# A graph attention layer on one core: address reads behind the copies, norms a round later, eight column tiles more

## The chip, the cores and the metric

The kernel runs on one core of a Trainium2 chip. The metric is the device time of one execution in microseconds (us), as the median of several runs; lower is better. A profiled execution gives the trace, whose span runs from the first to the last instruction of the core.

The engines are named as in the profile: PE (TensorE, matmuls), PEld (its weight loads), DVE (VectorE), ACT (ScalarE), POOL (GpSimd, which here issues the gathers) and SP (SyncE, which issues the plain transfers). ACTq, DVEq and SPq are the sequencers of these engines: they read instructions in order, carry out register reads themselves, and hand the rest to the engine.

## The reference: what is computed

One layer of attention over a graph of 6250 nodes with 206250 edges, sorted by their destination, 128 features in 8 heads of 16:

```python
Q, K, V = x @ WQ, x @ WK, x @ WV            # 6250 x 128 each
Eh = edge_attr @ WE                         # 206250 x 128
score = sum over d of K[src] * Q[dst] * Eh / 4      # per edge and head
score = exp(clip(score, -5, 5))
wV = segment_sum(V[src] * score, dst)       # per node
Z  = segment_sum(score, dst)
out = layernorm(x + wV / (Z + 1e-6))
```

## The kernel before

**Tiles and rounds.** Edges are cut into 1612 tiles of 128 (one edge a partition), tiles into 406 batches of four (the last ones smaller). After a start in which the tables K and V of all nodes are made and written to memory (`kv`), one loop over `b` (line 626) has one round per batch. From batch 12 on (`XB`) the order of instructions on each engine is that in which the program writes them (line 628, `manual_schedule`), so a round's place in a queue can be read off the loop's body.

**What a round does.** Gathers: `gather` (line 421) fetches for each tile the rows of K and V of its 128 source nodes, one indirect DMA a tile, issued by POOL (line 430), 256 floats a row, into one of twelve `kvrows` buffers. The first gather of a batch waits for a matmul of an earlier batch (line 434, `lag`, from 12 batches at first down to 3 at the end), so that gathers keep to the pace of TensorE. TensorE: `stage_a` multiplies the edge features by WE (`eps`, line 498) and picks the rows of Q with a one-hot matrix (`qps`, line 501). DVE: `stage_b` of the batch before multiplies K by Q (`kq`, line 508) and by the edge features (`kqe`, 511), sums over each head (`sc`, 514) and clips (517); one-hot matrices are built (470 and 483) for two batches at a time. ACT: `weigh` takes the exponential twice (524 to `msg`, 525 to `exp_p`). DVE: `messages` multiplies V by `exp_p` (558), a round after `weigh`. TensorE: `stage_c` adds the messages by destination with a one-hot matmul (578).

**Column tiles.** For a share of the tiles POOL issues no gather (line 425). Their 128 source columns of x, which lies transposed in SBUF (`xT_sb`, 128 features by 6250 nodes), are copied one by one into a tile `xcol`, and a matmul with WK and WV makes the rows (`project_columns`, line 412), which ACT puts in the place of the gathered ones (line 419). `column_tiles` (line 75) says which: one batch in 13/6 on average from batch 24 on, `COLP = (13, 6)`, 176 in all. Each such batch has three gathers instead of four.

The copies are in `columns` (line 372). ACT takes columns 0 to 79 in ten runs of eight (`COLA = (8, 10)`), one copy a column (line 403), DVE columns 80 to 127 in six runs of eight, two columns an instruction (`COLV = (8, 6)`, line 400), so four instructions a run. Where a column lies is only known at run time: each run is preceded by a read of eight addresses from SBUF to registers of that engine's sequencer (line 392). `addresses` holds what is read and not yet used. A call tops it up to two runs and then copies one, so the read in front of a run is that of the run behind it. `columns` is called for ACT twice a round (lines 651 and 685: the first up to half a round's share, ahead of `weigh`; the second behind it) and for DVE three times (663, 669, 675), a run each at most.

**Norms.** When the sums of two blocks of 128 nodes are complete, `finish` (line 542) issues matmuls that put them together (`finps`), and in the same round, behind `weigh`, ACT copies the result out (`fin`, line 551) and appends the steps of `layernorm` to `pending`. At the next round `pending` goes to `norms` (line 653), and `fill` (line 616) issues one step at a time, four times a round on DVE, after the steps that make Q's table (`qwork`). The first step (`rz`, line 791) reads `fin`. When all steps are issued the output store goes on SP two rounds later.

Of the kernel before, what the change touches and what calls it, by code (L numbers as in the profile page):

```python
# [18 lines left out]
N, E, D, H, DH = 6250, 206250, 128, 8, 16  # L19
# [30 lines left out]
QLOOK = 3  # L50
QREG = 16
COL0 = 24
COLP = (13, 6)
COLA = (8, 10)
COLV = (8, 6)
COLL = 8
# [3 lines left out]
XT_AT = RING + P  # L60
# [14 lines left out]
def column_tiles():  # L75

    last = LAST // B - 1
    n = (last - 2 - COL0 + COLL) * COLP[1] // COLP[0]
    return [B * min(COL0 + k * COLP[0] // COLP[1], last - (n - 1 - k)) + B - 1 for k in range(n)]

# [22 lines left out]
def edge_attention(ctx: ExitStack, tc: tile.TileContext, x, xT, srcT, srcC, dstT, dstB, dst0, bnd, lo, eaT,  # L103
                   wq, wkv, we, out, kv, qtab, qs, relD):
    nc = tc.nc
# [27 lines left out]
    nbat = len(batches)  # L133
    col_batches = [t // B for t in column_tiles()]
    col_half = (len(col_batches) + 1) // 2
    col_at = cp.tile([col_half, 2, P], I32, name="col_at")
# [4 lines left out]
    with ExitStack() as fast:  # L141
# [79 lines left out]
        def late_loads():  # L221
            if NT > C0:
                nc.sync.dma_start(src_sb[1], srcT[:, C0:])
                nc.sync.dma_start(dst_sb[:, C0:], dstT[:, C0:])
# [72 lines left out]
        xbs, stores, norms, pending, ready, finished, loaded_x = {}, [], [], [], [], [], set()  # L297
# [39 lines left out]
        def load_rel(c):  # L337
            if c in rels or c * RC >= NT:
                return
            n = min(RC, NT - c * RC) * P  # L340
            rels[c] = wp.tile([QROWS, RC * P], BF16, name="relb", bufs=2)
            nc.sync.dma_start(rels[c][:, :n], relD.rearrange("j e -> (j e)")[None, c * RC * P:c * RC * P + n]
                              .to_broadcast([QROWS, n]))
# [3 lines left out]
        def load_chunk(c):  # L347
            if c in chunks or c * CH >= NT:
                return
            n = min(CH, NT - c * CH) * P  # L350
            tl = ep.tile([P, CH * P], F32, name="ea", tag="ea")
            nc.sync.dma_start(tl[:, :n], eaT[:, c * CH * P:c * CH * P + n])
            chunks[c] = tl
# [16 lines left out]
        addresses, fetched = {}, {}  # L370

        def columns(eng, b, share=1.0, most=99):

            size, runs = COLA if eng is nc.scalar else COLV
            first = 0 if eng is nc.scalar else COLA[0] * COLA[1]
            engine = mybir.EngineType.Activation if eng is nc.scalar else mybir.EngineType.DVE
            copy = eng.copy if eng is nc.scalar else eng.tensor_copy
            due = int((b - COL0 + COLL - 1 + share) * runs * COLP[1] / COLP[0] + 1e-6)
            total = len(col_batches) * runs
            while copied.get(engine, 0) < min(due, total) and most:  # L380
                most -= 1
                k, j = divmod(copied.get(engine, 0), runs)
                copied[engine] = copied.get(engine, 0) + 1
                if k not in col_tiles:
                    col_tiles[k] = wp.tile([P, P], F32, name="xcol", bufs=XCOLS)
                to, j = col_tiles[k].bitcast(U8), first + j * size
                known = addresses.setdefault(engine, [])
                while len(known) < 2 and fetched.get(engine, 0) < total:
                    kf, jf = divmod(fetched.get(engine, 0), runs)
                    fetched[engine] = fetched.get(engine, 0) + 1  # L390
                    jf = first + jf * size
                    known.append(nc.values_load_multi_w_load_instructions(  # L392
                        col_at[kf % col_half:kf % col_half + 1, kf // col_half, jf:jf + size], engines=(engine,),
                        min_val=XT_AT, max_val=XT_AT + 8 * (N - 1) + 4,
                        skip_runtime_bounds_check_because="edges name nodes")[1])
                at = known.pop(0)
                if eng is nc.vector:
                    for c in range(0, size, 2):
                        both = [xT_bytes[:, ds(a - XT_AT, 8)] for a in at[c:c + 2]]
                        eng.tensor_tensor(to[:, 4 * (j + c):4 * (j + c) + 8], *both, op=ALU.bitwise_or)  # L400
                    continue
                for c in range(size):
                    copy(to[:, 4 * (j + c):4 * (j + c) + 4], xT_bytes[:, ds(at[c] - XT_AT, 4)])  # L403

        def project_columns(b):

            if b not in col_batches:
                return
            g = gathered[b]
            k = col_batches.index(b)  # L410
            pk = psT.tile([P, 2 * D], F32, name="colkv", tag="oT")
            nc.tensor.matmul(pk, col_tiles.pop(k), wkv_sb, start=True, stop=True)  # L412
            projected.append((g, pk))

        def place_columns():

            while projected:
                g, pk = projected.pop()
                nc.scalar.copy(g[:, B - 1, :], pk)  # L419
# [202 lines left out]
            elif norms and (not late or late.pop()) and next(norms[0], None) is None:  # L622
                norms.pop(0)

        held, late = [], []
        for b in range(nbat + 3):
            if b >= XB and not manual:
                manual.append(fast.enter_context(tc.manual_schedule()))
            held += [(b + SLAG, store) for store in stores]
            stores.clear()  # L630
            if held and (held[0][0] <= b or b >= nbat):
                held.pop(0)[1]()
            if b < nbat:
                load_chunk(batches[b][0] // CH + EB - 3)
                load_rel(batches[b][0] // RC + 1)
                load_q(batches[b][0] // WT + QLOOK)
                g = gathered.pop(b)
                if b == min(XB, nbat - 1):
                    late_loads()
                if b == min(XB + 8, nbat - 1):  # L640
                    relative(C0, NT)
                if b >= 30:
                    next(second_half, None)
                if b == 0:
                    for i in range(AHEAD):
                        stage_0(i)
                        stage_0t(i)
                stage_a(b, g)
                if b + GLEAD < nbat and b + GLEAD not in gathered:
                    gathered[b + GLEAD] = gather(b + GLEAD)  # L650
                columns(nc.scalar, b, 0.5)
            late[:] = [False] * 9 + [True] if b >= nbat - 2 else []
            norms.extend(pending)
            pending.clear()
            for j in ready:
                finish(j)
            ready.clear()
            steps = stage_b(b - 1) if 0 <= b - 1 < nbat else iter(())
            next(steps, None)
            if b + AHEAD < nbat and together(b + AHEAD):  # L660
                stage_0(b + AHEAD)
            if b < nbat:
                columns(nc.vector, b, 1.0, 1)
            fill()
            next(steps, None)
            if b + AHEAD < nbat and together(b + AHEAD):
                stage_0t(b + AHEAD)
            if b < nbat:
                columns(nc.vector, b, 1.0, 1)
            fill()  # L670
            next(steps, None)
            if 0 <= b - 2 < nbat:
                messages(b - 2)
            if b < nbat:
                columns(nc.vector, b, 1.0, 1)
            fill()
            next(steps, None)
            fill()
            place_columns()
            if 0 <= b - 1 < nbat:  # L680
                weigh(b - 1)
            while blocks_out:
                blocks_out.pop(0)()
            if b < nbat:
                columns(nc.scalar, b)
            if 0 <= b - 2 < nbat:
                stage_c(b - 2)
            if b < nbat:
                project_columns(b + GLEAD)
                build_q(q_built(min(NJ - 1, batches[b][0] // WT + QLOOK + 2)), True)  # L690
                if not qwork and len(built) < q_built(
                        min(NJ - 1, batches[min(nbat - 1, b + 3)][0] // WT + QLOOK + 2)):
                    qwork.append(q_rows(len(built)))
                    next(qwork[0])
                    fresh[:] = [0, 0, 0]
            if b == min(60, nbat):
                count_inside()
            if b == min(80, nbat + 1):
                inside = nc.values_load(cnt_i[0:1, 0:1], min_val=0, max_val=2 * EPAD,
                                        skip_runtime_bounds_check_because="two counts of EPAD edges")  # L700
# [158 lines left out]
```

## Time and profile before

| | us |
|---|---|
| median of three runs | 1847.12 (1847.1 to 1848.22) |
| the profiled execution, its own time | 1840.47 |
| its span | 1838.7 |
| mean granted clock of TensorE | 0.931 of full |

The profile page gives for each engine its busy time, its share of the span and its instructions; then the chain of work that ended last, followed back from the end, as shares by engine. Groups of instructions have the form: line, engine, operation, output <- input, shape, count | busy time, mean ns of one | idle time of the engine just ahead of them, and what ended most of it ("issue": nothing that the profile shows). Copies and other short instructions overlap on their engine, so busy time divided by count is less than the mean of one. The lists of waits give total us, how often, and the longest. The timelines give start and length in us, and in brackets the idle time ahead of an instruction with its releaser; equal instructions that follow each other are merged (x40). Busy time by window has one row a stretch, with the engines' busy time and instruction counts.

### The profile page before, as it was taken

The numbers are of one execution on the slowest core, as the hardware profiler recorded it, in microseconds if no ns is written. First come the engines' busy times: TensorE is split into PE (matmuls) and PEld (weight loads), VectorE is DVE, ScalarE is ACT, GpSimd is POOL, SyncE is SP. The second block draws the span as 40 slices with busy tenths as digits, with TensorE's granted clock in tenths as the row PEclk, the third lists the DMA queues.
The fourth block names the chain that finished last, engine by engine and source line by source line (L and its number), as shares of the span: only waits on it lengthen the run. The fifth ranks groups of instructions, "written<-read, shape, count | busy, mean of one in ns | idle before, by whom it ended". The sixth has DMA issues, their size and how long they took to land.

```text
span 1838.7 us, 48927 instructions
## 1 busy us (share of the span) xinstructions
PE 1299.2 (71%) x9130; PEld 1118.7 (61%) x9130; DVE 1720.6 (94%) x7478; ACT 1608.3 (87%) x15268; POOL 1375.8 (75%) x1443
## 2 busy tenths in 40 slices
PE   6886667676676777776777667766767667766776
PEld 4776656565665666665666556655656656655665
DVE  5579999999999999999999999999999999999998
ACT  2339889899999999999999999999999999999994
POOL 6777777777777777777777777777777777777774
PEclk8999899889989899999899999999999999899989
DMA  8776667676776577677667766866876676667762
GB/s 281 231 228 199 192 183 225 194 205 196 211 221 202 177 224 216 182 208 221 202 199 213 226 192 183 241 198 180 241 213 191 192 229 194 203 185 232 217 191 77
DMA packets 170631, 376.74 MB, mean 205 GB/s; under 512 B 58423, under 2 KB 84369, under 8 KB 170315
## 3 DMA queue, kind: packets, MB, share of 16 engines
q0 software_dynamic: 68144, 185.10, 35.0%
q1 hardware_dynamic: 101031, 187.38, 33.9%
q14 instruction: 242, 1.98, 0.3%
q8 instruction: 74, 1.21, 0.3%
q10 hardware_dynamic: 1140, 1.06, 0.2%
HBM read 358.60 MB, written 14.81 MB: 203 GB/s over the span
## 4 chain that ended last, share of the span: by engine, by line
DVE 42%; DMA 17%; ACT 13%; PE 11%; issue 6%; DVEq 5%; POOL 4%; ACTq 2%; SPq 0%; POOLq 0%
DMA kvrows<-kv,src 14%; ACT xcol L403 11%; DVE xcol L400 8%; DVE kqe L511 6%; DVE kq L508 6%; DVE sc L514 6%; POOL kvrows L430 4%; DVEq L392 4%; DVE onehot L470 4%; PE eps L498 4%; DVE msg L558 4%; PE agg L578 3%; DVE onehotT L483 2%; ACTq L392 2%; DMA dB_sb<-dstB 1%
## 5 line engine op out<-in xcount | busy, mean ns | idle before, releaser
L430 POOL DMA_INDIRECT kvrows<-kv,src x1388 | 1328.6, 957 | 423.0 <-issue 313.0
L403 ACT COPY xcol<-xT_sb 128x4 uint8 x14080 | 1422.3, 191 | 60.5 <-issue 54.2
L498 PE MATMUL eps<-we_sb,ea 128*128 128x128 f32 x3224 | 488.9, 298 | 384.8 <-issue 182.7
L498 PEld LDWEIGHTS eps<-we_sb,ea 128*128 128x128 f32 x3224 | 425.0, 205 | 482.6 <-issue 353.7
L578 PE MATMUL agg<-msg,onehot 128*128 128x136 f32 x3224 | 526.0, 310 | 109.4 <-DVE msg L558 101.1
L578 PEld LDWEIGHTS agg<-msg,onehot 128*128 128x128 f32 x3224 | 447.0, 208 | 165.6 <-DVE msg L558 152.2
L400 DVE TENSOR_TENSOR xcol<-xT_sb 128x8 uint8 x4224 | 416.1, 156 | 8.7 <-issue 4.6
L508 DVE TENSOR_TENSOR kq<-kvrows,qps 128x512 f32<-128x512 f32 x406 | 274.0, 675 | 35.2 <-PE qps L501 17.1
L558 DVE TENSOR_TENSOR msg<-kvrows,exp_p 128x512 f32<-128x512 f32 x406 | 271.1, 668 | 7.5 <-ACT exp_p L525 7.5
L511 DVE TENSOR_TENSOR kqe<-kq,eps 128x512 f32<-128x512 f32 x406 | 272.3, 671 | 3.1 <-PE eps L498 2.6
L514 DVE TENSOR_REDUCE sc<-kqe 128x32 f32<-128x512 f32 x406 | 270.2, 665 | 0.5
L501 PE MATMUL qps<-qw,onehotT 126*128 126x128 bf16 x1612 | 166.6, 227 | 0.0
L524 ACT ACTIVATE msg<-sc 128x32 f32<-128x32 f32 x406 | 92.6, 228 | 72.0 <-DVE sc L517 64.5
L470 DVE TENSOR_TENSOR onehot<-iota_p,dst_sb 128x512 f32<-128x512 f32 (+2 forms) x206 | 137.5, 668 | 2.0 <-PE agg L578 2.0
L501 PEld LDWEIGHTS <-onehotT 126*128 126x128 bf16 x1612 | 132.9, 102 | 8.2
L412 PE MATMUL colkv<-wkv_sb,xcol 128*128 128x256 f32 x352 | 114.2, 409 | 0.8 <-ACT xcol L403 0.8
L483 DVE TENSOR_SCALAR onehotT<-relb,node 126x1024 bf16<-126x1024 bf16 (+2 forms) x206 | 100.0, 486 | 3.3 <-DMA relb<-relD 2.0
L517 DVE TENSOR_SCALAR sc<-sc 128x32 f32<-128x32 f32 x406 | 82.1, 202 | 0.3
L525 ACT ACTIVATE exp_p<-sc 128x32 f32<-128x32 f32 x406 | 73.7, 182 | 0.0
L419 ACT COPY kvrows<-colkv 128x256 f32<-128x256 f32 x176 | 63.8, 362 | 0.3 <-PE colkv L412 0.3
L430 POOL DMA_INDIRECT kvrows<-x,src x48 | 46.3, 964 | 22.5 <-issue 11.6
L412 PEld LDWEIGHTS colkv<-wkv_sb,xcol 128*128 128x128 f32 x352 | 59.7, 209 | 1.0 <-ACT xcol L403 1.0
(76 smaller groups left out, 537.3 us busy)
## 6 DMA issues: line engine op xcount, KB each, us to landing
ea<-eaT SPq DMA_DIRECT2D x201, 512.0 KB
relb<-relD SPq DMA_DIRECT2D x100, 504.0 KB
kvrows<-kv,src POOLq DMA_INDIRECT x1388
qw<-qs SPq DMA_DIRECT2D x202, 31.5 KB
kv<-kvst SPq DMA_DIRECT2D x12, 512.0 KB
qs<-qst SPq DMA_DIRECT2D x48, 96.0 KB
xst<-xT SPq DMA_DIRECT2D x12, 256.0 KB
xb<-x SPq DMA_DIRECT2D x24, 128.0 KB
```

The lines of the kernel that those rows point to most:

```text
L400: eng.tensor_tensor(to[:, 4 * (j + c):4 * (j + c) + 8], *both, op=ALU.bitwise_or)
L403: copy(to[:, 4 * (j + c):4 * (j + c) + 4], xT_bytes[:, ds(at[c] - XT_AT, 4)])
L412: nc.tensor.matmul(pk, col_tiles.pop(k), wkv_sb, start=True, stop=True)
L430: ins = nc.gpsimd.indirect_dma_start(out=g[:k, i, :f], out_offset=None, in_=rows, in_offset=bass.IndirectOffsetOnAxis(ap=src_col(t)[:k], a ...
L470: nc.vector.tensor_tensor(tl[:, HW:].rearrange("p (t n) -> p t n", n=P)[:, :n, :HW], iota_p[:, None, :].to_broadcast([P, n, HW]), rel[:, t ...
L498: nc.tensor.matmul(pe[:, i, :], ea[:, i * P:i * P + P], we_sb, start=True, stop=True)
L501: expanded[b] = nc.tensor.matmul(pq[:, i, :], ohT[:, i * P:i * P + P], loaded[t0 // WT], start=True, stop=True)
L508: nc.vector.tensor_tensor(t0[:, :n], g[:, :n, :D], pq[:, :n], op=ALU.mult)
L511: nc.vector.tensor_tensor(t1[:, :n], t0[:, :n], pe[:, :n], op=ALU.mult)
L514: nc.vector.tensor_reduce(sc[:, :n], t1[:, :n].rearrange("p b (h d) -> p b h d", h=H), axis=AX.X, op=ALU.add)
L558: nc.vector.tensor_tensor(m[:, :n, :D].rearrange("p b (h d) -> p b h d", h=H), g[:, :n, D:].rearrange("p b (h d) -> p b h d", h=H), exp_p[ ...
L578: nc.tensor.matmul(aggs[k][:, 0], oh[0][:, oh[1] + i * P:oh[1] + i * P + P], m[:, i, :], start=not final and t % (QUAD * G) == 0, stop=tail)
```

## The change

There are three edits, in `columns`, in the loop, and in one constant.

1. The share of column tiles goes from 6 batches in 13 to 15 in 31. By `column_tiles` this gives 184 tiles, where the old constant gives 176; the change's own short description says 183.
2. ACT's address reads: a call tops up to one run (which only reads something in the very first run), copies, and then reads the addresses of the next run. DVE keeps two.
3. A norm whose `fin` was copied in round b goes to `norms` at round b + 2 instead of b + 1, by way of a list `waiting`; in the last rounds (from `nbat - 3` on) it goes at once.

```diff
-COLP = (13, 6)
+COLP = (31, 15)
...
-                while len(known) < 2 and fetched.get(engine, 0) < total:
...
+                def fetch(ahead):
+                    while len(known) < ahead and fetched.get(engine, 0) < total:
...
+                fetch(2 if eng is nc.vector else 1)
                 at = known.pop(0)
                 if eng is nc.vector:
...
                 for c in range(size):
                     copy(to[:, 4 * (j + c):4 * (j + c) + 4], xT_bytes[:, ds(at[c] - XT_AT, 4)])
+                fetch(1)
...
-        held, late = [], []
+        held, late, waiting = [], [], []
...
-            norms.extend(pending)
+            norms.extend(waiting)
+            waiting[:] = pending
             pending.clear()
+            if b >= nbat - 3:
+                norms.extend(waiting)
+                waiting.clear()
```

More of the change, by code (lines that the diff above doesn't have):

```diff
@@ L387, in columns @@
                 known = addresses.setdefault(engine, [])
-                while len(known) < 2 and fetched.get(engine, 0) < total:
[L389 to L395, printed above, removed]
+                def fetch(ahead):
+                    while len(known) < ahead and fetched.get(engine, 0) < total:
+                        kf, jf = divmod(fetched.get(engine, 0), runs)
+                        fetched[engine] = fetched.get(engine, 0) + 1
+                        jf = first + jf * size
+                        known.append(nc.values_load_multi_w_load_instructions(
+                            col_at[kf % col_half:kf % col_half + 1, kf // col_half, jf:jf + size],
+                            engines=(engine,), min_val=XT_AT, max_val=XT_AT + 8 * (N - 1) + 4,
+                            skip_runtime_bounds_check_because="edges name nodes")[1])
+                fetch(2 if eng is nc.vector else 1)
                 at = known.pop(0)
```

## Prediction

> **What bounds the kernel now.** I began with the page, first with its busy times and the chain that ended last.
>
> ```profile
> PE 1299.2 (71%) x9130; PEld 1118.7 (61%) x9130; DVE 1720.6 (94%) x7478; ACT 1608.3 (87%) x15268; POOL 1375.8 (75%) x1443
> DVE 42%; DMA 17%; ACT 13%; PE 11%; issue 6%; DVEq 5%; POOL 4%; ACTq 2%; SPq 0%; POOLq 0%
> ```
>
> DVE looks like the bound, and POOL, at 75%, looks free. It isn't. The waits of POOL between 138 and 1790 us (the stage in which column tiles are made) show why: 30 different releasers, all with the same longest wait. The two largest:
>
> ```profile
> POOL kvrows L430 <- issue: 294.7, 967, 0.3
> POOL kvrows L430 <- DVE xcol L400: 18.9, 62, 0.3
> ```
>
> No gather ever waited over 0.3 us, whoever is named as its releaser. So the 0.3 us is a fixed cost between two gathers, and the names are coincidence. The timeline of POOL says the same in the middle and at the very end:
>
> ```profile
> 956.44 0.95 POOL L430 DMA_INDIRECT kvrows<-kv,src  x1 [0.30 <-issue]
> 957.70 0.95 POOL L430 DMA_INDIRECT kvrows<-kv,src  x1 [0.30 <-issue]
> ...
> 1808.53 0.95 POOL L430 DMA_INDIRECT kvrows<-kv,src  x1 [0.30 <-PE agg L578]
> 1811.03 0.95 POOL L430 DMA_INDIRECT kvrows<-kv,src  x1 [0.30 <-issue]
> 1821.04 0.91 POOL L430 DMA_INDIRECT kvrows<-kv,src  x1 [0.30 <-PE agg L578]
> ```
>
> A gather takes a slot of 1.26 us (957.70 - 956.44), and the slots follow each other without a hole to 1822 us, 17 us before the end. POOL is a queue that is full from beginning to end.
>
> DVE is the second bound. Batch 208 has its first multiply (kq) at 984.41, batch 400 at 1814.09; their last gathers are the rows at 957.70 and 1811.03 above.
>
> ```profile
> 984.41 0.67 DVE L508 TENSOR_TENSOR kq<-kvrows,qps 128x512 f32<-128x512 f32 x1
> 1814.09 0.69 DVE L508 TENSOR_TENSOR kq<-kvrows,qps 128x512 f32<-128x512 f32 x1
> ```
>
> POOL's lead is 26.7 us at batch 208 and 3.1 us at batch 400. DVE is the faster of the two by little, lives off a head start of the gathers, and has used it up just as the work ends. The busy times by stage fit (the first row is the whole column stage):
>
> ```profile
> core 0: us, PE busy (x) PEld busy (x) DVE busy (x) ACT busy (x) POOL busy (x), PEclk, DMA share, GB/s
> 138.00:1790.00 1652.00, 1162.42 (x8305) 1008.27 (x8303) 1595.02 (x7116) 1539.79 (x14932) 1253.13 (x1309) 0.93 0.70 205
> 900.00:1100.00 200.00, 141.22 (x1025) 121.59 (x1023) 195.97 (x882) 190.50 (x1858) 151.84 (x159) 0.95 0.72 212
> 1700.00:1790.00 90.00, 65.00 (x442) 56.61 (x440) 84.18 (x382) 84.72 (x826) 68.06 (x73) 0.89 0.71 204
> ```
>
> DVE is busy 98% in the middle and 94% at the end, where it waits for gathers. ACT has 112 us without work in 1652. What DVE and ACT wait for in the same stage:
>
> ```profile
> DVE kq L508 <- PE qps L501: 16.8, 28, 1.0
> DVE rz L791 <- ACT fin L551: 15.7, 16, 2.5
> DVE kq L508 <- DMA kvrows<-kv,src: 6.5, 6, 1.8
> ...
> ACT xcol L403 <- issue: 52.1, 184, 0.9
> ACT msg L524 <- DVE sc L517: 37.9, 58, 4.5
> ACT fin L551 <- PE finps L537: 10.9, 9, 2.4
> ```
>
> Only 6.5 us of DVE's time is waiting for gathered rows. With a POOL that never held it, DVE would end about 6.5 us sooner; with a DVE that cost nothing, POOL would still end where it does. So there are two sums, one for each, and the later decides.
>
> **The change part by part.** The instruction order of the changed kernel has 184 column projections, where the old one has 176 (352 matmul passes, two each). So 8 tiles more are filled by copies, and 8 gathers are gone.
>
> **POOL.** 8 slots of 1.26 us: 10.1 us. Nothing stands between the slots, so POOL ends 10.1 us sooner if nobody holds it back. Its first gathers are the same.
>
> **DVE, more columns.** A column tile has 6 runs of 4 instructions on DVE (48 columns, 2 an instruction, 4 instructions behind one address read), so 48 runs more.
>
> ```profile
> L400 DVE TENSOR_TENSOR xcol<-xT_sb 128x8 uint8 x4224 | 416.1, 156 | 8.7 <-issue 4.6
> ...
> 1003.64 0.68 DVE L558 TENSOR_TENSOR msg<-kvrows,exp_p 128x512 f32<-128x512 f32 x1
> 1004.24 0.39 DVE L400 TENSOR_TENSOR xcol<-xT_sb 128x8 uint8 x4
> 1004.54 0.17 DVE L517 TENSOR_SCALAR sc<-sc 128x32 f32<-128x32 f32 x1
> ```
>
> Start to start a run costs 0.30 us here (1004.24 to 1004.54); by the busy time it is 416.1/1056 = 0.39 us, of which some overlaps its neighbours. I take 0.33, nearer the row without overlap: 48 x 0.33 = 15.8 us (14.4 to 18.9). All of it lies on DVE's path, which has no holes. It is more than POOL gains: by this edit alone DVE would be late by 15.8 - 6.5 = 9.3 us.
>
> **DVE, the norms a round later.** The first instruction of a block's norm (rz, line 791) stands in DVE's queue one round behind the matmuls that finish the block, and reads a copy that ACT makes behind the exponentials of that round:
>
> ```profile
> 1385.64 0.19 ACT L525 ACTIVATE exp_p<-sc 128x32 f32<-128x32 f32 x1
> ...
> 1385.94 0.39 ACT L551 COPY fin<-finps 128x272 f32<-128x272 f32 x1
> 1386.36 0.17 DVE L791 TENSOR_SCALAR rz<-fin 128x16 f32<-128x16 f32 x1 [0.31 <-ACT fin L551]
> ...
> 1388.10 0.67 DVE L558 TENSOR_TENSOR msg<-kvrows,exp_p 128x512 f32<-128x512 f32 x1
> ```
>
> Sixteen of the 24 waited, 15.7 us in all, the longest 2.5 us. A round is 4.3 us (984.41 to 1814.09 is 829.7 us for 192 rounds), so one round more covers the longest wait, and the 15.7 us go: -15.7. The output stores behind the norms move a round later on SP's queue too, behind loads of a later round; no instruction before the end waits for a store, and the last rounds hand norms over at once as before. No cost. The bounds: -15.7, if ACT's lateness then meets no other instruction, and 0, if it does (third rival).
>
> **ACT, more columns.** 80 copies a tile:
>
> ```profile
> L403 ACT COPY xcol<-xT_sb 128x4 uint8 x14080 | 1422.3, 191 | 60.5 <-issue 54.2
> L419 ACT COPY kvrows<-colkv 128x256 f32<-128x256 f32 x176 | 63.8, 362 | 0.3 <-PE colkv L412 0.3
> ```
>
> 8 x 80 x 1422.3/14080 = 64.6 us and 8 x 0.36 = 2.9 us: 67.5 us into 112 us of idle time. 44 us are left, 39 after the span has shrunk by 5. But 52.1 us of the 112 are gaps ahead of the copies ("issue"), which are no free time unless the reads that cause them are hidden.
>
> **ACT, the address reads.** One such gap, with the reads of ACT's sequencer in the same window:
>
> ```profile
> 1051.20 0.23 ACT L524 ACTIVATE msg<-sc 128x32 f32<-128x32 f32 x1 [0.55 <-DVE sc L517]
> 1051.33 0.18 ACT L525 ACTIVATE exp_p<-sc 128x32 f32<-128x32 f32 x1
> 1051.83 4.05 ACT L403 COPY xcol<-xT_sb 128x4 uint8 x40 [0.31 <-issue]
> ...
> L392 ACTq TENSOR_LOAD <-col_at x1: 547/547/547, 1051.2 to 1051.2; - x1
> L392 ACTq TENSOR_LOAD <-col_at x1: 547/547/547, 1052.0 to 1052.0; - x1
> ```
>
> ACT had caught up, the sequencer had nothing queued, and the read of 0.55 us stood in front of copies whose addresses had been there for long. The second read, at 1052.0, shows no gap: 40 copies in 4.05 us is 0.10 each with four more reads between them. There eight copies (0.8 us) were queued ahead of the read. Behind the change the first eight copies follow the exponentials at once, and the first read has those eight to hide behind, as the second has now. The copies of a run then need a read that has only just ended, where today one whole run lies between; since the sequencer is held for the whole 0.55 us either way, I count no more for it. So the 52.1 us fall to near 0 (0 to 52.1 kept for the range). ACT keeps 39 us of slack, 2%.
>
> The Trainium skill (Advanced Engine Details and Errata, Sequencer and Instruction Queues, Sequencer Loop) says that further engine instructions can be read and queued while a control instruction executes. By that rule the read wouldn't hold the copies, the gap would have another cause and would stay where it is, and the sum would be that of the fourth case below; the row at 1051.83 speaks against it, since the copies start just when the read that began at 1051.2 has ended.
>
> **What tight ACT costs DVE.** DVE's msg multiply needs ACT's exponentials of the round before. The whole span has 7.5 us of that wait:
>
> ```profile
> DVE msg L558 <- ACT exp_p L525: 7.5, 10, 1.3
> ```
>
> With ACT at 98% it will come up now and then: I take 1, between 0 and 7.5.
>
> **The sum.** DVE: +15.8 - 15.7 - 6.5 (gathers are 10.1 us sooner, none of the six waits is over 1.8) + 1.0 = -5.4 us. POOL: -10.1 us. DVE is the later: span 1838.7 - 5.4 = 1833.3. The profiled execution took 1840.47 us, 1.8 over its span; the median of the three runs is 1847.12, 8.4 over it. I put the difference on the median: **1841.7 us**, 0.3% faster.
>
> **The rivals.** A difference under 0.2%, 3.7 us, can hardly be told from none.
>
> Second case: POOL stays the bound. It needs DVE to save over 4.7 us more, for instance from the 16.8 us of kq on qps (28 rounds in which DVE is too short for TensorE; a run more in the round covers 0.3 of a wait). For it speaks that DVE waits for rows at the end; against it, that the added runs fall into those rounds only by chance. Time: 1847.1 - 10.1 = 1837.0.
>
> Third case: the wait only moves. rz waits because ACT is late, and an ACT with 67.5 us more work stays late; what rz doesn't wait, msg waits half a round on. For it: ACT's slack shrinks to 2%. Against it: in the rows above exp_p was done 0.5 us before fin (1385.83 to 1386.33), and msg on DVE starts 1.7 us behind rz. All of it back: 15.8 - 6.5 = +9.3, 1856.4; half back: 1848.6. I write 1849.
>
> Fourth case, the slower side: the reads still show, and ACT becomes the bound. Place: each of the 1840 reads. It decides from 39/1840 = 0.02 us a read on; above that every further 0.01 us costs 18 us. With today's 52.1 us kept, ACT needs 1540 + 67.5 + 52.1 + 10.9 (its wait for finps) = 1670 us in a stage of 1652: +18, 1865 us. For it: ACT is near full and the slack is thin. Against it: the gapless 40 copies.
>
> **How the numbers follow.** The forecast 0.50, of which 0.42 faster by over 0.2% and 0.08 within it; POOL the bound 0.17, faster; the wait moves 0.20, 0.13 within and 0.07 slower; ACT the bound 0.13, slower. Faster 0.59, same 0.21, slower 0.20. The range reaches from just under POOL's floor, 1836.5, to 1852, which holds half of the wait come back and the dear end of the runs (18.9 and 7.5 in the sum give +4.2, 1851.3). It leaves out the fourth case and the upper third of the third: just under 0.2.
>
> **What would show it.** Right: rz no longer waits for fin; "issue" ahead of ACT's copies is under 10 us; gathers still come every 1.26 us, 1380 from kv; DVE's wait for kvrows is near 0 and POOL's lead at batch 400 is over 3.1 us. Wrong: msg waits for exp_p by more than 7.5 us in all (third); ACT 99% busy, or gaps inside long rows of copies (fourth); POOL waits above 0.3 us, which would mean that buffers or the pace set by TensorE hold it and its 10.1 us are not to be had; a mean gather above 0.957 us.

## The result, and the profile after

The changed kernel takes 1842.14 us (median of 11 runs, 1839.2 to 1846.08), the kernel before 1847.12 us (11 runs). The ratio is 0.9972, 95% interval 0.9964 to 0.9979: 5.0 us faster. The profiled execution took 1842.14 us, just its median, with a span of 1840.4; that of before, with 1838.7, had been 6.6 us under its own median. So the two profiles can't be subtracted span from span, and what follows compares what each shows inside.

The page of the changed kernel: the chain that ended last by engine, and the groups of gathers and of ACT's copies.

```profile
DVE 51%; DMA 16%; PE 9%; issue 7%; DVEq 5%; POOL 5%; SPq 0%; ACT 0%; POOLq 0%
...
L435 POOL DMA_INDIRECT kvrows<-kv,src x1380 | 1330.3, 964 | 420.9 <-issue 306.7
L407 ACT COPY xcol<-xT_sb 128x4 uint8 x14720 | 1446.1, 191 | 2.6 <-issue 2.1
```

ACT had 13% of the chain and ACTq 2%; both are gone, and the idle time ahead of ACT's copies is 2.6 us, where it was 60.5. The gathers are 1380, eight fewer, but POOL's busy time did not fall: 1330.3 us against 1328.6, since the mean gather took 964 ns here and 957 in the other profile.

The waits between 138 and 1790 us in the changed kernel, by engine:

```profile
POOL kvrows L435 <- issue: 286.6, 940, 0.3
POOL kvrows L435 <- DVE kq L513: 13.4, 44, 0.3
...
POOL kvrows L435 <- DVE onehotT L488: 1.1, 3, 0.5
```

```profile
DVE kq L513 <- PE qps L506: 12.3, 23, 1.9
DVE kq L513 <- DMA kvrows<-kv,src: 7.7, 10, 1.8
```

```profile
ACT msg L529 <- DVE sc L522: 49.6, 77, 6.1
...
ACT xcol L407 <- issue: 1.6, 5, 0.6
```

One gather waits 0.5 us; apart from it, POOL still never waits over 0.3 us. rz no longer stands in DVE's list. ACT's "issue" gaps went from 52.1 us to 1.6, and what ACT waits for now is DVE.

POOL's lead at batches 208 and 400, by the last gather of the batch and its kq, and the last gather of all:

```profile
956.70 0.95 POOL L435 DMA_INDIRECT kvrows<-kv,src  x1 [0.30 <-issue]
...
1810.81 0.95 POOL L435 DMA_INDIRECT kvrows<-kv,src  x1 [0.30 <-issue]
...
1820.85 0.91 POOL L435 DMA_INDIRECT kvrows<-kv,src  x1 [0.30 <-PE finps L542]
```

```profile
979.89 0.69 DVE L513 TENSOR_TENSOR kq<-kvrows,qps 128x512 f32<-128x512 f32 x1
...
1814.42 0.69 DVE L513 TENSOR_TENSOR kq<-kvrows,qps 128x512 f32<-128x512 f32 x1
```

23.2 us and 3.6 us: the same picture as before (26.7 and 3.1). DVE lives off the lead and has used it up at the end.

### The profile page after: what moved, and what is told of

Read it like the earlier page. It is cut to its first block, busy times and chain, and to the rows that moved or that the text cites. A ratio compares the mean times of both kernels' runs of the same rounds, so it can differ in the third digit from the quotient of the medians.

```text
span 1840.4 us, 49895 instructions
## 1 busy us (share of the span) xinstructions
PE 1303.0 (71%) x9146; PEld 1126.8 (61%) x9146; DVE 1733.8 (94%) x7670; ACT 1638.7 (89%) x15916; POOL 1377.4 (75%) x1435
## 4 chain that ended last, share of the span: by engine, by line
DVE 51%; DMA 16%; PE 9%; issue 7%; DVEq 5%; POOL 5%; SPq 0%; ACT 0%; POOLq 0%
DMA kvrows<-kv,src 15%; DVE xcol L404 11%; DVE kqe L516 8%; DVE kq L513 8%; DVE sc L519 7%; DVEq L394 5%; POOL kvrows L435 5%; DVE onehot L475 5%; DVE msg L563 4%; PE eps L503 4%; DVE onehotT L488 3%; PE agg L583 3%; DVE sc L522 1%; DMA dB_sb<-dstB 1%; PE finps L542 1%
## 5 line engine op out<-in xcount | busy, mean ns | idle before, releaser
L435 POOL DMA_INDIRECT kvrows<-kv,src x1380 | 1330.3, 964 | 420.9 <-issue 306.7
L407 ACT COPY xcol<-xT_sb 128x4 uint8 x14720 | 1446.1, 191 | 2.6 <-issue 2.1
L404 DVE TENSOR_TENSOR xcol<-xT_sb 128x8 uint8 x4416 | 437.7, 158 | 10.8 <-issue 7.0
L417 PE MATMUL colkv<-wkv_sb,xcol 128*128 128x256 f32 x368 | 120.6, 412 | 0.0
L424 ACT COPY kvrows<-colkv 128x256 f32<-128x256 f32 x184 | 67.8, 369 | 7.4 <-issue 1.5
L417 PEld LDWEIGHTS colkv<-wkv_sb,xcol 128*128 128x128 f32 x368 | 63.8, 213 | 0.0
```

The costliest lines, as they stand in the source:

```text
L435: ins = nc.gpsimd.indirect_dma_start(out=g[:k, i, :f], out_offset=None, in_=rows, in_offset=bass.IndirectOffsetOnAxis(ap=src_col(t)[:k], a ...
```

## The experiments

Two theories. Theory 1 is the prediction: DVE ends about 5 us after POOL in the changed kernel, and sets the time. Theory 2, formed from the profile after: POOL's queue sets the time alone, before and after, and what varies is how long a gather takes.

The runs fell on six chips. On three of them the kernel before takes 1843 to 1848 us, as it did for the prediction; on the other three it takes 2460 to 2500 us and another engine sets the end. So the runs that answer the question are the first three here, and the nine others are told after them.

### Eight gathers less, nothing added (e5)

```diff
+                if i == 1 and b % 44 == 0 and 0 < b < 396:
+                    nc.sync.dma_start(g[:, i, :], kv[b * 8:b * 8 + P])
+                    continue
```

This leaves out eight gathers of the changed kernel; plain loads of other rows stand in for them.

> The changed kernel, but in 8 batches one gather of four is replaced by a plain load of 128 consecutive rows of kv, issued by SP (other rows than the reference wants; the same bytes and shapes). POOL has 8 slots less, nothing is added to DVE or ACT. Theory 1 (the prediction): DVE ends 4.7 us later than POOL in the changed kernel, so taking 10.1 us more off POOL gives nothing: 0 to -1 us against the changed kernel, ratio to the kernel before 0.997. Theory 2: POOL's queue is full from end to end and sets the time alone: -10 us more, ratio to the kernel before 0.992 (0.991 to 0.993).

Measured: 1832.31 us against 1845.13 of the kernel before on that chip, ratio 0.9927 (0.9913 to 0.9940). Against the changed kernel that is 0.9927/0.9972, 8 us less (5 to 11 by the two intervals). The page's gathers, the last of them in the timeline, waits of POOL and DVE between 138 and 1790 us, and the kq of batch 400:

```profile
L438 POOL DMA_INDIRECT kvrows<-kv,src x1372 | 1319.7, 962 | 422.1 <-issue 302.9
```

```profile
1813.18 0.90 POOL L438 DMA_INDIRECT kvrows<-kv,src  x1 [0.30 <-DMA kvrows<-kv,src]
```

```profile
POOL kvrows L438 <- PE qps L509: 16.4, 50, 1.4
...
POOL kvrows L438 <- PE eps L506: 6.1, 13, 2.5
```

```profile
DVE kq L516 <- PE qps L509: 9.5, 20, 1.0
DVE kq L516 <- DMA kvrows<-kv,src: 6.8, 4, 2.9
```

```profile
1806.07 0.69 DVE L516 TENSOR_TENSOR kq<-kvrows,qps 128x512 f32<-128x512 f32 x1 [0.70 <-DMA kvrows<-kv,src]
```

The last gather is 7.7 us sooner than in the changed kernel (1820.85), and the end 8.1 us sooner (span 1832.3). DVE does the same work as in the changed kernel and began batch 400 at 1806.07 instead of 1814.42, 8.4 us sooner. Its last instruction ends 6.7 us sooner; the other 1.4 us at the end lie behind the work (the next section comes back to them). Theory 1 gave 0 to -1; it falls. POOL sets the end of the changed kernel. Its queue was not quite full here: five gathers in this stage waited over 0.3 us, up to 2.5, some 4 us in all beyond the usual 0.3.

### Reads and norms without the tiles (e10)

```diff
-COLP = (31, 15)
+COLP = (13, 6)
```

> The reads behind the copies and the norms a round later with 176 column tiles, on a chip where the kernel before takes 1845 us. Theory 1 (the prediction): DVE ends 6.5 us before POOL in the kernel before, so a DVE with 15.7 us less to wait changes nothing: ratio 0.999 to 1.001. Theory 2 (POOL's queue alone sets the end; its slots are longer where DVE holds POOL up): 0.999 to 1.003, POOL never waits over 0.3 us, and the mean of a gather is 0.957 to 0.964 us. Theory 3 (the chip's pace in the kernel before is set by DVE or ACT after all): the time falls by 5 us or more, 0.997 or less.

Measured: 1847.68 us against 1847.56, ratio 0.9995 (0.9981 to 1.0009): nothing. From its page, its waits in the column stage and its timelines (the last gather of batch 208 and its kq):

```profile
L435 POOL DMA_INDIRECT kvrows<-kv,src x1388 | 1337.4, 964 | 423.2 <-issue 311.0
```

```profile
DVE kq L513 <- DMA kvrows<-kv,src: 21.1, 21, 2.2
DVE kq L513 <- PE qps L506: 17.6, 33, 1.2
```

```profile
961.58 0.95 POOL L435 DMA_INDIRECT kvrows<-kv,src  x1 [0.30 <-issue]
```

```profile
970.16 0.69 DVE L513 TENSOR_TENSOR kq<-kvrows,qps 128x512 f32<-128x512 f32 x1
```

DVE did become faster: at batch 208 it had brought POOL's lead down to 8.6 us, where the kernel before still had 26.7. From there it runs at POOL's pace and waits for rows 21.1 us in the column stage, where the kernel before waits 6.5. A faster DVE meets a full queue earlier and gains nothing, as both theories had it.

### The reads back in front, with the tiles (e11)

```diff
-                fetch(2 if eng is nc.vector else 1)
+                fetch(2)
...
-                fetch(1)
```

> The changed kernel with ACT's reads back in front of the copies (184 tiles, norms a round later), on a chip where the kernel before takes 1845 us. Theory 1 (the prediction's fourth case): with its 52 us of gaps ACT needs 1670 us in the column stage of 1652 and becomes the bound: +18 us over before, ratio 1.010, and DVE's msg waits for exp_p by over 10 us. Theory 2: a gap opens only where ACT had caught up and would have waited anyway, so ACT absorbs most of them: ratio 0.997 to 1.000, gaps of 30 to 55 us in all, msg's wait for exp_p under 12 us, POOL never over 0.3 us.

Measured: 1839.13 us against 1843.58, ratio 0.9980 (0.9969 to 0.9990); the intervals of this run and of the changed kernel (0.9964 to 0.9979) overlap. Its waits, ACT's in the column stage and DVE's over the whole span, and its gathers:

```profile
ACT xcol L407 <- issue: 29.6, 107, 1.2
```

```profile
DVE msg L562 <- ACT exp_p L529: 7.9, 10, 1.5
```

```profile
L434 POOL DMA_INDIRECT kvrows<-kv,src x1380 | 1325.9, 961 | 421.5 <-issue 312.0
```

The gaps are back, but only 29.6 us of them: a gap opens only when ACT has caught up, and with eight tiles more it does so less often (ahead of msg it waits for DVE's sc 17 times in this stage, 58 times in the kernel before). DVE waits hardly longer for the exponentials than before (7.5 us). Against both theories' 0.3 us, one gather waited 1.3 us for TensorE. The fourth case of the prediction, +18 us, is refuted on these chips: by the two intervals, the place of the reads is worth at most about 0.2% of the time with 184 tiles.

### On chips where the kernel before takes 2460 to 2500 us (e1 to e4, e6 to e9, e12)

e1 and e9 are the kernel before with no edit.

> The kernel before, unchanged, for a second profile: the first profiled execution (1840.5 us) lies 6.6 us under the median of its timed runs (1847.1). Theory 1 (the prediction): DVE and POOL end about 6.5 us apart, a gather's slot is a constant 1.26 us, so a run of 1847 us shows the extra time as waits of DVE, with the same 1.262 us a gather. Theory 2: POOL's queue of gathers alone sets the end and its slots are not constant: a run of 1847 us shows a mean slot of 1.266 us and more gathers over 1.0 us busy (over 90 where the first profile has 63), and POOL still never waits over 0.3 us. Ratio 1.000 by both.

> The kernel before, unchanged, for a second profile beside runs of about 1845 us. Theory 1: a constant slot of 1.262 us a gather, and the 5 us over the first profile are waits of DVE. Theory 2: the 5 us are in the slots: a mean of about 1.265 us and over 80 gathers busy for over 1.0 us, where the first profile has 63.

Measured: ratios 1.0029 (1.0000 to 1.0058) and 1.0008 (0.9977 to 1.0038). Both asked for a profile of a run of about 1845 us and met chips on which there is none, so they don't answer. What they show is another bound. From e1, the chain, ACT's copies, a piece of ACT's timeline, and one of POOL's waits:

```profile
ACT 49%; issue 24%; DVE 6%; ACTq 6%; PE 6%; another core or an unknown queue 3%; POOL 2%; DMA 2%; DVEq 1%; POOLq 0%; SPq 0%
...
L403 ACT COPY xcol<-xT_sb 128x4 uint8 x14080 | 1504.0, 190 | 578.8 <-issue 569.3
```

```profile
1007.59 0.23 ACT L524 ACTIVATE msg<-sc 128x32 f32<-128x32 f32 x1
1008.24 0.20 ACT L525 ACTIVATE exp_p<-sc 128x32 f32<-128x32 f32 x1 [0.42 <-issue]
```

```profile
POOL kvrows L430 <- PE qps L501: 344.6, 169, 7.2
```

On such a chip ACT is held up for 569 us ahead of its copies, by nothing that the profile shows. It isn't the address reads alone: between the two exponentials at 1007.59 and 1008.24 stands no read, and there are 0.42 us. POOL now waits up to 7.2 us for the pace set by TensorE. By the chain, with ACT at 49%, the whole pipeline goes at ACT's pace.

e2 has the tiles alone (`COLP = (31, 15)` in the kernel before), e4 is the kernel of e11, e3 and e8 that of e10.

> Only the 184 column tiles; the reads stand in front and the norms come a round earlier, as before. Theory 1: DVE pays 15.8 us for the runs and gets only the 6.5 us of gather waits back: +9.3 us, ratio 1.005; ACT with its 52 us of gaps may add to it, up to 1.010. Theory 2: POOL has 8 slots less, DVE keeps the 15.7 us of rz waits and runs out of lead: between -5 and +8 us, ratio 0.997 to 1.004. Both: rz waits for fin again.

> The changed kernel with ACT's reads back in front of the copies (184 tiles, norms a round later). Theory 1: ACT needs 1670 us in the column stage of 1652 and becomes the bound: about +18 us over before, ratio 1.010, msg on DVE waits for exp_p by over 10 us. Theory 2: ACT's gaps of about 50 us come back, but a gap comes only where ACT had caught up and waits anyway, so they cost little: 0 to +5 us over the changed kernel, ratio 0.997 to 1.000.

> The reads behind the copies and the norms a round later, but 176 column tiles as before. Theory 1: DVE would end 22 us sooner than POOL, POOL keeps its 1436 slots: no change, ratio 0.999 to 1.001, with DVE's wait for kvrows up by some 15 us. Theory 2: the same time, ratio 0.999 to 1.001, and a lead of POOL at batch 400 that cannot fall under about 3 us. If the time falls by over 3 us, both are wrong on what bounds the kernel before.

> The reads behind the copies and the norms a round later with 176 column tiles, once more, on a chip where the kernel before takes 1845 us. Theory 1: no change (0.999 to 1.001), since POOL keeps its 1436 slots. Theory 2: no gain, and if the steadier DVE puts onehotT beside more gathers, up to +5 us, 1.000 to 1.003: then the number of gathers over 1.0 us is above 80.

Measured: e2 1.0187 (1.0154 to 1.0220), e4 1.0146 (1.0115 to 1.0177), e3 0.9988 (0.9963 to 1.0014), e8 on another of these chips 0.9945 (0.9921 to 0.9969). Where ACT sets the pace, the tiles cost 1.9% alone and 1.5% together with the later norms. The reads and norms together were worth nothing on one chip and 0.5% on the other. The changed kernel itself didn't run on such a chip.

e12 has 191 tiles, in hope of a version faster than both.

```diff
-COLP = (31, 15)
+COLP = (2, 1)
```

> The changed kernel with one column tile in every second batch, COLP = (2, 1): 191 column tiles instead of 184. POOL has 7 slots less (-8.8 us), DVE 42 runs more (+13.9 us), ACT 59 us more. Theory 1 (the prediction: DVE ends after POOL in the changed kernel): 14 us slower than the changed kernel, ratio to the kernel before 1.005. Theory 2 (POOL's queue sets the end, and DVE and ACT still have room): up to 8.8 us faster than the changed kernel, ratio 0.992 to 0.997, with POOL's lead at batch 304 larger than 7 us. If ACT is full before that: ACT busy over 1630 us of the 1652, POOL waits over 0.3 us or DVE's msg waits for exp_p by over 15 us, ratio 0.998 or more.

Measured: 1.0248 (1.0210 to 1.0285), on a chip of the second kind, with ACT's copies as in e1:

```profile
L407 ACT COPY xcol<-xT_sb 128x4 uint8 x15280 | 1605.0, 190 | 477.6 <-issue 463.3
```

It says that more tiles cost more where ACT is the bound. Whether 191 tiles are faster where POOL is, wasn't measured.

e6 and e7 ask what makes a gather long. In the changed kernel 107 gathers are busy for over 1.0 us, and 83 of these lie beside an onehotT of DVE, of which there are 206; in the profile of before it is 47 of 63. One of them, and the gather behind it:

```profile
657.06 0.47 DVE L488 TENSOR_SCALAR onehotT<-relb,node 126x1024 bf16<-126x1024 bf16 x1
657.18 1.18 POOL L435 DMA_INDIRECT kvrows<-kv,src  x1 [0.30 <-issue]
...
658.67 0.95 POOL L435 DMA_INDIRECT kvrows<-kv,src  x1 [0.30 <-PE qps L506]
```

e6 replaces the four DVE instructions of a run by one, so that the columns DVE fills are not the right ones; e7 does the same and makes onehotT otherwise:

```diff
-            nc.vector.tensor_scalar(ohT[:, :n * P], rels[t0 // RC][:, e0:e0 + n * P], node[:QROWS], None,
-                                    op0=ALU.is_equal)
+            nc.vector.tensor_tensor(ohT[:, :n * P], rels[t0 // RC][:, e0:e0 + n * P],
+                                    node[:QROWS].to_broadcast([QROWS, n * P]), op=ALU.is_equal)
```

> The changed kernel with one DVE instruction a column run instead of four (the 48 columns of each column tile that DVE fills are not the right ones; the address reads stay). DVE has over 250 us less to do. Theory 1 (the prediction): the changed kernel waits for DVE, so the time falls to POOL's end, 4.7 us under the changed kernel, ratio to the kernel before 0.9945. Theory 2: POOL's queue sets the end already and DVE's work is not on it: 0 to -2 us against the changed kernel, ratio 0.996 to 0.997, with DVE waiting for kvrows by over 150 us.

> As the run with one DVE instruction a column run, and onehotT made by a tensor_tensor with a broadcast operand instead of a tensor_scalar (the same values; about 0.6 us longer each, which DVE now has to spare). Of the gathers that were busy for over 1.0 us in the changed kernel, 83 of 107 lie beside an onehotT. Theory 2: onehotT in its fast form holds the port through which POOL writes a gather's descriptors, and the gathers beside it are longer; without that form under 40 gathers are over 1.0 us and the time falls by 15 to 25 us against the run with onehotT as it is: ratio to the kernel before 0.983 to 0.989. Theory 1, and any theory in which the long gathers are chance: the same time as that run within 2 us, and about 100 gathers over 1.0 us.

Measured: 1.0075 (1.0039 to 1.0111) and 0.9941 (0.9909 to 0.9973). The times belong to ACT's pace and don't bear on the question (e7 is faster than e6 although its gathers are longer; why is open); the lengths of the gathers do. e6, then e7 with its onehotT:

```profile
L434 POOL DMA_INDIRECT kvrows<-kv,src x1380 | 1318.7, 956 | 1054.8 <-issue 514.4 <-PE qps L505 330.7 <-remote 87.5
```

```profile
L434 POOL DMA_INDIRECT kvrows<-kv,src x1380 | 1385.8, 1004 | 964.5 <-issue 478.3 <-PE qps L505 273.3 <-remote 85.2
...
L487 DVE TENSOR_TENSOR onehotT<-relb,node 126x1024 bf16<-126x1024 bf16 (+2 forms) x206 | 245.9, 1194 | 3.7 <-PE xtps L449 2.2 <-PE qps L505 1.5
```

I had expected fewer long gathers, under 40. There are 155 in e7, 140 of them beside onehotT, and 77 in e6, 64 of them beside it. The operation is 1194 ns long in e7 (508 in e6), and the mean gather went from 956 to 1004 ns. So it doesn't take the fast form (the tensor_scalar) to hold POOL up; onehotT does so in both forms, and more in that of e7. The two runs don't separate whether that comes from its length or from its second input in SBUF. The changed kernel's own trace speaks for the inputs: beside DVE's msg (0.67 us, one of its two inputs in PSUM) gathers take 950 ns in the mean, and 1 of 483 is over 1.0 us; beside the norms' `h` (0.41 us, both inputs in SBUF) they take 1005 ns, and 12 of 38 are (from 138 us on, gathers beside an onehotT left out). The Trainium skill (SBUF — State Buffer, Who interferes with whom) says that a DVE instruction with two SBUF inputs contends with a GpSimd instruction that reads SBUF, and that one in a two-port mode, which a tensor_scalar can enter, contends with GpSimd too. The longer gathers of e7, whose onehotT has two inputs in SBUF, agree with the first; which mode the onehotT of e6 is in, no run shows.

## Why the prediction was right, and where it was not

**The time was right, by a step that was wrong.** Forecast 1841.7, measured 1842.14. The forecast had DVE end 5.4 us sooner and POOL 10.1, and took "DVE is the later". Shown by e5: POOL is the later. The second case of the prediction, POOL stays the bound, names the right mechanism, and its time, 1837.0, is 5 us too low. That the forecast came within 0.5 us is luck: POOL's queue, the later one, gave about half of its 10.1 us, which happens to be near the 5.4 us of the sum for DVE.

**POOL's queue is full from end to end: right.** In the column stage no gather of before or e10 waited over 0.3 us, and one of the changed kernel did (0.5 us).

**"8 slots of 1.26 us: 10.1 us": mis-sized.** It came to 5.0 us by the medians. The count of slots is right; their length is not a constant of the program. The mean gather was 957 ns (before), 964 (changed), 964 (e10), 961 (e11) and 962 (e5), and 7 ns on 1380 gathers are 9.7 us, as much as the eight slots. Most of it lies beside onehotT: the gathers that overlap one take 986 ns in the mean before and 1020 in the changed kernel, all others 952 and 954. Long gathers go from 63 to 107 in the two profiles; e10, with 176 tiles, has 99. Eight more slots taken away in e5, with no column work added, gave 8 us, of which 1.4 lie behind the work. Whether the changed kernel's gathers are longer than those of a typical run of the kernel before stays open: its only profile on such a chip is of a run 6.6 us under its median, and e10, with 176 tiles, has 964 ns too. By an estimate from these numbers, 6.6 us over 1435 slots put a median run of the kernel before at 957 + 4.6, some 962 ns; the remaining 2 ns are 3 of the missing 5 us. That is argued, not shown.

Another 1.3 us are lost behind the work, where the prediction has no term. From the end of DVE's last instruction to the end of the span are 5.3 us in the profile of before and 6.6 in that of the changed kernel. SP's 14 closing instructions take 1.5 us in the first and 2.8 in the second, with 1.2 us between two of them for which the profile shows no cause:

```profile
L855 SPq EVENT_SEMAPHORE  x14: 17/28/28, 1837.1 to 1838.6; - x14
```

```profile
L864 SPq EVENT_SEMAPHORE  x14: 17/28/28, 1837.5 to 1840.3; - x14
```

Nine of the ten profiles with the norms a round later have 6.5 to 6.7 us there (e5 has 5.2), the four without that edit 5.2 to 5.4. It goes with that edit in all but e5; what makes it is open. Without it the eight slots would have given some 6.3 us, by an estimate from the medians and these two profiles.

**DVE's column runs, +15.8: about right as work, not on the path.** DVE's busy time rose from 1720.6 to 1733.8 us. The step that failed is the sum for DVE, -5.4 us, which made DVE the later. It charged the runs in full to a path "which has no holes", and took the 6.5 us of waiting for rows as all that DVE had to spare. The path has holes. In the column stage kq waits for TensorE's qps 16.8 us before and 17.6 in e10, with 176 tiles, and 12.3, 10.0 and 9.5 us in the changed kernel, e11 and e5, with 184: the added runs fill part of these waits, as the second case had asked for. So DVE still waits 7.7 us for rows in the changed kernel, where the prediction had near 0, and in e5 the same DVE work ended sooner and DVE still waited 6.8 us for rows. Its waits for rows are only the least that it had to spare. In the last quarter (lead 8.7 us at batch 304 in the profile of before, 7.2 in that of the changed kernel) DVE follows POOL.

**The norms, -15.7: right in the trace, worth nothing alone.** rz doesn't wait in the changed kernel; the wait didn't move to msg (its wait for exp_p is 7.4 us over the whole span, 7.5 before), so the third case is refuted. By e10 the norms and reads together give 0.9995. Whether the tiles would gain without the norms wasn't measured on a chip of the first kind.

**The reads: the mechanism right, and not needed.** 52.1 us of gaps became 1.6. At a place where ACT had to wait for DVE, in the timeline of the changed kernel:

```profile
194.23 0.23 ACT L529 ACTIVATE msg<-sc 128x32 f32<-128x32 f32 x1 [0.75 <-DVE sc L522]
194.37 0.18 ACT L530 ACTIVATE exp_p<-sc 128x32 f32<-128x32 f32 x1
194.49 4.02 ACT L407 COPY xcol<-xT_sb 128x4 uint8 x40
```

The copies follow the exponentials at once, with the reads hidden behind the first eight. The Trainium skill's rule that instructions are queued while a control instruction executes (Advanced Engine Details and Errata, Sequencer and Instruction Queues, Sequencer Loop) would have kept the gap; for these reads the trace disagrees with it. ACT's added work was smaller than forecast, +30 us of busy time (1608.3 to 1638.7) instead of +67.5: a copy costs 1446.1/14720 = 98 ns of busy time where it had 101. The fourth case then had the wrong price: e11 keeps the reads in front and loses nothing that can be told.

**The chances.** The gain of 0.28% is over the bound of 0.2%, as forecast with 0.59; the range held the time. Of the signs for being right, four came out (rz, the 1.6 us ahead of ACT's copies, 1380 gathers, a lead over 3.1 us at batch 400) and one did not, the wait for rows (7.7 us, not near 0). Of those for being wrong two came: a mean gather above 957 ns, and one wait of POOL above 0.3 us.

## What to carry to other kernels

When a queue shows the same small wait ahead of every entry, whoever is named as its releaser, it is full, and its engine can be the bound even at 75% busy: try taking entries off it, and don't rank it by its share. An engine that catches up with such a queue looks 98% busy and nearly unstalled; the sum of its waits for the queue is only the least that it has to spare, since work added to it also fills its other waits, and an experiment that relieves the queue alone tells the two apart. And before two profiles are subtracted, look where each profiled run lies among the timed ones: here that difference, 6.6 us, was larger than the effect.

## What the runs showed of the hardware that was not expected

The same program takes 1847 us on some chips and 2460 to 2500 us on others, at a granted TensorE clock of 0.92 to 0.94 and of 0.75 to 0.79. On the latter ACT, with 15268 short instructions, has 569 us of gaps that nothing in the profile explains, some between two instructions with no read between them; what makes them late is open. The sign of the tile edit differs between the two kinds: the same kernel with 184 tiles gave 0.9980 on the first (e11) and 1.0146 on the second (e4).

A gather on POOL is mostly 0.94 to 0.95 us, and up to 1.3 us beside a DVE onehotT of 0.47 us (in the changed kernel five gathers behind 138 us are longer, up to 1.6 us, and none of them lies beside an onehotT). So a DVE instruction whose result no gather needs can lengthen POOL's queue. e7 shows it by experiment, on a chip where ACT sets the pace; where POOL's queue sets the time, it is read from the overlap alone.
